# A message-passing layer on one core: hand order for VectorE and ScalarE too, both chunks' results written in their own pair, and the node-span product in two halves

## The chip, the core and the metric

The kernel runs on one core of a Trainium2 chip. The metric is the device time of one execution in microseconds. The core has TensorE (matrix products; a weight load, PEld in the profile, and a product, PE, are separate instructions), VectorE (DVE), ScalarE (ACT), GpSimd (POOL) and SyncE (SP). SP and ACT also issue ordinary DMAs, POOL issues the indirect ones. Products land in PSUM, which has eight banks of 2 KB per partition; everything else works in SBUF, which has 128 partitions.

## The reference

One layer of a graph network with 12,500 nodes, 32 features and 400,000 edges that are sorted by their destination:

```python
edge_index = jnp.stack([src, dst])
h = jnp.maximum(_layernorm(x, axis=-1), 0.0)
x = x + _L0_gnn_ref(h, edge_index, edge_attr_32, W1, b1, W2, b2)

# inside _L0_gnn_ref(x, ...), where x is h:
e_feat = jnp.concatenate([x[rol], x[col], edge_attr], axis=-1)   # rol = src, col = dst
h = jax.nn.relu(e_feat @ W1 + b1)                                # 96 -> 64
v = h @ W2 + b2                                                  # 64 -> 32
x_cand = jax.ops.segment_max(v, col, num_segments=num_nodes)
return jnp.maximum(x_cand, x[:, -v.shape[-1]:])
```

## The kernel before

The edges are cut into four stripes of 100,000 (`NS`), and each stripe into 196 chunks of 512 (`NCH`, `C`). A chunk index `c` means 512 edges of each of the four stripes, side by side on the partitions. The loop at L94 takes two chunks per turn; one turn is called a pair here, and there are 98.

For one pair the work is:

- **Source rows.** `gather(c)` (L139) fetches the rows `h[src]` by indirect DMAs on POOL, one for each 128 edges: 12 per chunk in nearly all chunks. The remaining 512 edges of a chunk get their rows from TensorE: `rows_by_matmul` (L278) builds one-hot matrices from node keys on DVE (`hot`, seven instructions at L285; `its`, one at L287) and multiplies them with the node table that lies in SBUF in two parts (`hs`). One **row tile** is one product at L292 and fourteen at L295, over 448 columns, into a bank of `pv`; DVE reduces it to rows by a maximum (L297, `gm`). There are four row tiles per chunk, so eight per pair, made for the chunks of the next pair. In this text the row tiles of a pair in the new order are called a0 to a3 and b0 to b3.
- **Features to partitions.** `to_features` (L322) transposes both kinds of rows into `ht` on DVE (L324 for gathered rows, L326 for computed ones). L324 is what frees a `gh` buffer for a later gather; there are six, three pairs' worth.
- **Hidden layer.** `into_ph` (L379) adds three groups of products into four banks `ph`: the edge attributes `ea`, a one-hot of the destination window `of` times the rows `qw` of node products, and `ht`. ScalarE applies bias and relu (L389, `hid`).
- **Second layer.** L399 makes `pv[0]` and `pv[1]`, the messages of the two chunks, and a scan on DVE (L404, `sm`) runs a maximum along the edges that starts anew at each node.
- **Leaving.** `leave_1` turns `sm` by four transposes (L336, `tr`), adds the bias (L338, `so`), and marks the last edge of each node in a window of 32 nodes per stripe (L340, `last`). `leave_2` multiplies the two (L350), so that the maxima fall on their nodes, copies the result on ScalarE (L353, `wo`) and writes it by four DMAs on SP (L357).

`load(c)` brings attributes, destinations and breaks of four chunks at a time and the `qw` rows (L318), two chunks ahead.

PSUM is full: four banks for `ph`, one for `tr`, and three for `pv`. The three `pv` banks go round in the order of allocation, over row tiles and messages alike:

```python
po = ps.tile([P, C], F32, name="pv", bufs=3)[:, :D * A0]
pv = [ps.tile([P, C], F32, name="pv", bufs=3) for x in range(2)]
```

Within the loop the order of instructions on SP and TensorE is that of the program (`manual_schedule` at L273). On DVE, ScalarE and POOL a planner chooses the order when the kernel is built; in the trace it runs L324 two pairs ahead of the pair that uses it. On every engine instructions then run in their fixed order, each waiting for its semaphores. The row tiles are strewn between the other products by `next(tiles)`, and the chunk c - 1 of the pair before leaves in the middle of a pair, beside chunk c.

Of the kernel before, what the change touches and what calls it, by code (L numbers as in the profile page):

```python
# [20 lines left out]
DVE = mybir.EngineType.DVE  # L21

P = 128
# [35 lines left out]
def gnn_kernel(ctx, tc, x, src, src_mm, src_t, dst, dst_next, dst_ext, lo, hi, edge_attr, weights, w1, w2, b2, out):  # L59
# [212 lines left out]
    with tc.tile_pool(name="edges", bufs=3) as pool, tc.tile_pool(name="edges_ps", bufs=1, space=PSUM) as ps, \  # L272
            tc.manual_schedule(engines={SP, PE}):  # L273
        loaded = {}
        windows = {}
        mm_rows = {}

        def rows_by_matmul():  # L278

            for i, c in enumerate(MMC):  # L280
                kb = pool.tile([P, 2, MM * P], F16, name="kb", bufs=2)
                nc.scalar.dma_start(kb, ap(key_d, i * MM * P, [[0, P], [len(MMC) * MM * P, 2], [1, MM * P]]))
                hot = pool.tile([P, A1, MM * P], F32R, name="hot", bufs=2)
                for k in range(A1):
                    nc.vector.tensor_scalar(hot[:, k], kb[:, 0], key_p[:, k:k + 1], None, op0=ALU.is_equal)  # L285
                its = pool.tile([P, MM * P], BF16, name="its", bufs=2)
                nc.vector.tensor_scalar(its, kb[:, 1], place, None, op0=ALU.is_equal)  # L287
                gm = mm_rows[c] = pool.tile([P, MM, D], F32, name="gm", bufs=6)
                for m in range(MM):
                    e = slice(m * P, (m + 1) * P)  # L290
                    po = ps.tile([P, C], F32, name="pv", bufs=3)[:, :D * A0]
                    nc.tensor.matmul(po, its[:, e], others.rearrange("p f a -> p (f a)"), start=True, stop=False)  # L292
                    for k in range(A1):
                        for part in range(2):
                            nc.tensor.matmul(po, hot[:, k, e], hs[:, part, k].rearrange("p f a -> p (f a)"),  # L295
                                             start=False, stop=(k == A1 - 1 and part == 1))
                    nc.vector.tensor_reduce(gm[:, m, :], po.rearrange("p (f a) -> p f a", a=A0),  # L297
                                            axis=AX.X, op=ALU.max)
                    yield
# [20 lines left out]

        def to_features(c, gh):
# [9 lines left out]

# [14 lines left out]
        def leave_2(c, so, last):  # L346
# [8 lines left out]
            for s in range(NS):  # L355
                g = slice(s * W, (s + 1) * W)
                nc.sync.dma_start(top_d[s % 2][bass.ds(base[s], W), :], wo[g, s * D:(s + 1) * D])  # L357
# [213 lines left out]
```

## Time and profile before

| | us |
|---|---|
| median of 3 runs | 5318.59 |
| lowest, highest | 5317.23, 5335.30 |
| profiled execution | 5227.3 (its span: 5225.5) |

| engine | busy us | share of span |
|---|---|---|
| TensorE products | 3638.2 | 70% |
| TensorE weight loads (beside products) | 2775.9 | 53% |
| POOL | 2238.9 | 43% |
| VectorE | 1846.3 | 35% |
| ScalarE | 315.6 | 6% |

The mean granted TensorE clock is 0.81 of the full one. The setup before the loop takes about 180 us of the span. A row of the profile names the line, the engine, the operation, the tiles it writes and reads, and how long the engine stood idle before it with what ended the wait; "issue" there means that it waited for nothing that the profile shows, "remote" that it names no instruction that ended the wait.

### The profile page before, as it was taken

The numbers are of one execution on the slowest core, as the hardware profiler recorded it, in microseconds if no ns is written. First come the engines' busy times: TensorE is split into PE (matmuls) and PEld (weight loads), VectorE is DVE, ScalarE is ACT, GpSimd is POOL, SyncE is SP. The second block draws the span as 40 slices with busy tenths as digits, with TensorE's granted clock in tenths as the row PEclk, the third lists the DMA queues.
The fourth block names the chain that finished last, engine by engine and source line by source line (L and its number), as shares of the span: only waits on it lengthen the run. The fifth ranks groups of instructions, "written<-read, shape, count | busy, mean of one in ns | idle before, by whom it ended". The sixth has DMA issues, their size and how long they took to land. (4 is left out here: it accounts for less than half of the span.)

```text
span 5225.5 us, 57318 instructions
## 1 busy us (share of the span) xinstructions
PE 3638.2 (70%) x20281; PEld 2775.9 (53%) x20281; DVE 1846.3 (35%) x3612; ACT 315.6 (6%) x627; POOL 2238.9 (43%) x2369
## 2 busy tenths in 40 slices
PE   2376767676767676767676767676767676777687
PEld 1255555555555555555554555555555555555565
DVE  2333333333333333333333333333333333333344
ACT  1000000000000000000000000000000000000000
POOL 6534344444444444444444444444444444444420
PEclk6587878787878787878788888787878787878788
DMA  3321112211211121112111211121112211211121
GB/s 123 90 58 43 42 39 58 44 41 40 58 42 41 40 56 44 40 40 56 44 40 40 57 44 40 40 56 44 41 40 57 44 41 40 57 44 40 40 53 65
DMA packets 235577, 256.47 MB, mean 49 GB/s; under 512 B 123653, under 2 KB 211861, under 8 KB 222102
## 3 DMA queue, kind: packets, MB, share of 16 engines
q10 hardware_dynamic: 74084, 137.60, 9.7%
q0 software_dynamic: 75296, 38.70, 5.6%
q1 hardware_dynamic: 85906, 76.48, 4.9%
q8 instruction: 159, 2.61, 0.2%
q14 instruction: 132, 1.08, 0.1%
HBM read 238.44 MB, written 14.04 MB: 48 GB/s over the span
## 5 line engine op out<-in xcount | busy, mean ns | idle before, releaser
L143 POOL DMA_INDIRECT gh<-h_d,src_i x2353 | 2234.8, 950 | 2812.1 <-DVE ht L324 2098.3
L295 PE MATMUL pv<-hs,hot 128*128 128x448 f32 x10808 | 2874.0, 413 | 712.6 <-issue 712.4
L295 PEld LDWEIGHTS pv<-hs,hot 128*128 128x128 f32 x10808 | 2282.8, 212 | 1444.9 <-issue 1270.9
L297 DVE TENSOR_REDUCE gm<-pv 128x32 f32<-128x448 f32 x772 | 481.2, 623 | 2548.3 <-remote 1529.4
L292 PE MATMUL pv<-others,its 128*128 128x448 bf16 x772 | 301.9, 391 | 427.0 <-issue 386.0
L285 DVE TENSOR_SCALAR hot<-kb,key_p 128x512 fp32r<-128x512 f16 x1351 | 555.8, 479 | 9.5 <-DMA qw<-q_d 9.5
L350 PE MATMUL tr<-so,last 128*128 128x128 f32 x1568 | 250.2, 282 | 250.0 <-issue 240.8
L404 DVE TENSOR_TENSOR_SCAN sm<-pb,sm,pv 128x512 f32<-128x512 bf16 x195 | 248.9, 1276 | 469.3 <-remote 332.5
L350 PEld LDWEIGHTS tr<-so,last 128*128 128x128 f32 x1568 | 227.1, 197 | 229.5 <-issue 211.8
L389 ACT ACTIVATE hid<-ph,wt 128x512 f32<-128x512 f32 x392 | 239.3, 690 | 973.5 <-PE ph L379 529.9
L292 PEld LDWEIGHTS <-its 128*128 128x128 bf16 x772 | 78.0, 101 | 400.5 <-issue 387.4
L353 ACT ACTIVATE wo<-tr 128x128 f32<-128x128 f32 x196 | 54.5, 278 | 3810.7 <-remote 1817.6
L336 PE MATMUL tr<-ident,sm 128*128 128x128 f32 x784 | 146.0, 319 | 22.3 <-ACT wo L353 22.3
L336 PEld LDWEIGHTS tr<-ident,sm 128*128 128x128 f32 x784 | 117.9, 167 | 57.9 <-ACT wo L353 38.4
L338 DVE TENSOR_TENSOR so<-tr,wt 128x512 f32<-128x512 f32 x196 | 133.9, 683 | 24.1 <-PE pv L292 11.5
L340 DVE TENSOR_TENSOR last<-iota_w,at 128x512 f32<-128x512 f32 x196 | 131.6, 672 | 28.2 <-PE tr L350 28.2
L324 DVE STREAM_TRANSPOSE ht<-gh 128x384 f32<-128x384 f32 (+1 forms) x196 | 102.9, 563 | 71.0 <-PE ph L379 54.8
L379 PE MATMUL ph<-ea,wt 32*64 32x512 f32 x1568 | 110.0, 617 | 8.4 <-DMA ea<-in_edge_attr 8.4
L379 PE MATMUL ph<-ht,wt 32*64 32x512 f32 x1568 | 110.9, 612 | 0.5 <-issue 0.4
L379 PE MATMUL ph<-of,qw 32*64 32x512 f32 x1568 | 105.5, 592 | 6.2 <-issue 6.2
L399 PE MATMUL pv<-hid,wt 64*32 64x512 f32 x1568 | 108.9, 604 | 0.2 <-ACT hid L389 0.2
L287 DVE TENSOR_SCALAR its<-kb,place 128x512 bf16<-128x512 f16 x193 | 69.6, 361 | 96.4 <-remote 80.1
(68 smaller groups left out, 399.3 us busy)
## 6 DMA issues: line engine op xcount, KB each, us to landing
ea<-in_edge_attr SPq DMA_DIRECT2D x49, 1024.0 KB
db<-in_dst_ext ACTq DMA_DIRECT2D x196, 256.0 KB
kb<-key_d ACTq DMA_DIRECT2D x193, 256.0 KB
gh<-h_d,src_i POOLq DMA_INDIRECT x2353
pb<-pen_d ACTq DMA_DIRECT2D x196, 128.0 KB
qw<-q_d SPq DMA_DIRECT2D x784, 8.0 KB
top_d<-wo SPq DMA_DIRECT2D x784, 4.0 KB
top_d<-zero ACTq DMA_DIRECT2D x2, 1568.0 KB
```

Source lines behind the costliest of these rows:

```text
L143: nc.gpsimd.indirect_dma_start(out=gh[:, k, :], out_offset=None, in_=h_d[:, :], in_offset=bass.IndirectOffsetOnAxis(ap=src_i[:, c, k:k + 1 ...
L285: nc.vector.tensor_scalar(hot[:, k], kb[:, 0], key_p[:, k:k + 1], None, op0=ALU.is_equal)
L292: nc.tensor.matmul(po, its[:, e], others.rearrange("p f a -> p (f a)"), start=True, stop=False)
L295: nc.tensor.matmul(po, hot[:, k, e], hs[:, part, k].rearrange("p f a -> p (f a)"), start=False, stop=(k == A1 - 1 and part == 1))
L297: nc.vector.tensor_reduce(gm[:, m, :], po.rearrange("p (f a) -> p f a", a=A0), axis=AX.X, op=ALU.max)
L336: nc.tensor.transpose(px[:, j, :], sm[:, j * P:(j + 1) * P], ident)
L338: nc.vector.tensor_tensor(so, px, b2r[:, None, :].to_broadcast([P, J, P]), op=ALU.add)
L340: nc.vector.tensor_tensor(last, iota_w[:, None, None, :].to_broadcast([P, J, NS, W]), at[:, :, c * J:(c + 1) * J].rearrange("p s j -> p j ...
L350: nc.tensor.matmul(pw, last[:, j].rearrange("p s w -> p (s w)"), so[:, j, :], start=(j == 0), stop=(j == J - 1))
L379: nc.tensor.matmul(ph[s][x * HID:(x + 1) * HID], w[g], e[g], start=start, stop=stop)
L389: nc.scalar.activation(hid[s], ph[s], AF.Relu, bias=b1c)
L404: nc.vector.tensor_tensor_scan(sm, loaded.pop(c + x)[2], pv[x], before, op0=ALU.add, op1=ALU.max)
```

## The change

DVE and ScalarE join SP and TensorE in the hand order, so that their instructions run as the loop is written. The generator `rows_by_matmul` becomes three functions: `load_keys` (the DMA of keys, on ScalarE's queue), `one_hots` (the eight DVE instructions, in whole or in part) and `tile_by_matmul` (the products), which hands its reduction back to be placed later by `select()`. `of` and `last` get functions of their own, `window_hots` and `lasts`. In the loop the gathers stand ahead of the loads, each reduction has its place after a row tile, and both chunks of a pair leave in that pair. The product in `leave_2` covers, instead of 128 by 128 with only the diagonal blocks used, two halves of 64 by 64 columns into two halves of the partitions; the copy to `wo` is 64 columns wide. `sm` has three buffers instead of four.

```diff
@@ -19,6 +19,7 @@
 SP = mybir.EngineType.SP
 PE = mybir.EngineType.PE
 DVE = mybir.EngineType.DVE
+ACT = mybir.EngineType.Activation
 
 P = 128
 N = 12500
@@ -270,33 +271,48 @@
 
     ea_v = edge_attr.rearrange("s f e -> (s f) e")
     with tc.tile_pool(name="edges", bufs=3) as pool, tc.tile_pool(name="edges_ps", bufs=1, space=PSUM) as ps, \
-            tc.manual_schedule(engines={SP, PE}):
+            tc.manual_schedule(engines={SP, PE, DVE, ACT}):
         loaded = {}
         windows = {}
+        ofs = {}
+        keys = {}
+        hots = {}
         mm_rows = {}
 
-        def rows_by_matmul():
-
-            for i, c in enumerate(MMC):
-                kb = pool.tile([P, 2, MM * P], F16, name="kb", bufs=2)
-                nc.scalar.dma_start(kb, ap(key_d, i * MM * P, [[0, P], [len(MMC) * MM * P, 2], [1, MM * P]]))
-                hot = pool.tile([P, A1, MM * P], F32R, name="hot", bufs=2)
-                for k in range(A1):
-                    nc.vector.tensor_scalar(hot[:, k], kb[:, 0], key_p[:, k:k + 1], None, op0=ALU.is_equal)
-                its = pool.tile([P, MM * P], BF16, name="its", bufs=2)
-                nc.vector.tensor_scalar(its, kb[:, 1], place, None, op0=ALU.is_equal)
-                gm = mm_rows[c] = pool.tile([P, MM, D], F32, name="gm", bufs=6)
-                for m in range(MM):
-                    e = slice(m * P, (m + 1) * P)
-                    po = ps.tile([P, C], F32, name="pv", bufs=3)[:, :D * A0]
-                    nc.tensor.matmul(po, its[:, e], others.rearrange("p f a -> p (f a)"), start=True, stop=False)
-                    for k in range(A1):
-                        for part in range(2):
-                            nc.tensor.matmul(po, hot[:, k, e], hs[:, part, k].rearrange("p f a -> p (f a)"),
-                                             start=False, stop=(k == A1 - 1 and part == 1))
-                    nc.vector.tensor_reduce(gm[:, m, :], po.rearrange("p (f a) -> p f a", a=A0),
-                                            axis=AX.X, op=ALU.max)
-                    yield
+        def load_keys(c):
+            if c in MMC:
+                kb = keys[c] = pool.tile([P, 2, MM * P], F16, name="kb", bufs=2)
+                nc.scalar.dma_start(kb, ap(key_d, (c - MMC.start) * MM * P,
+                                           [[0, P], [len(MMC) * MM * P, 2], [1, MM * P]]))
+
+        def one_hots(c, groups):
+
+            if c not in MMC:
+                return
+            if c not in hots:
+                hots[c] = (pool.tile([P, A1, MM * P], F32R, name="hot", bufs=2),
+                           pool.tile([P, MM * P], BF16, name="its", bufs=2))
+            hot, its = hots[c]
+            for k in groups:
+                nc.vector.tensor_scalar(hot[:, k], keys[c][:, 0], key_p[:, k:k + 1], None, op0=ALU.is_equal)
+            if A1 - 1 in groups:
+                nc.vector.tensor_scalar(its, keys.pop(c)[:, 1], place, None, op0=ALU.is_equal)
+
+        def tile_by_matmul(c, m):
+            if c not in MMC:
+                return
+            if m == 0:
+                mm_rows[c] = pool.tile([P, MM, D], F32, name="gm", bufs=6)
+            hot, its = hots[c]
+            e = slice(m * P, (m + 1) * P)
+            po = ps.tile([P, C], F32, name="pv", bufs=3)[:, :D * A0]
+            nc.tensor.matmul(po, its[:, e], others.rearrange("p f a -> p (f a)"), start=True, stop=False)
+            for k in range(A1):
+                for part in range(2):
+                    nc.tensor.matmul(po, hot[:, k, e], hs[:, part, k].rearrange("p f a -> p (f a)"),
+                                     start=False, stop=(k == A1 - 1 and part == 1))
+            rows = mm_rows[c][:, m, :]
+            return lambda: nc.vector.tensor_reduce(rows, po.rearrange("p (f a) -> p f a", a=A0), axis=AX.X, op=ALU.max)
 
         def load(c):
             if c % LOAD == 0:
@@ -318,6 +334,10 @@
                 nc.sync.dma_start(qw[s * W:(s + 1) * W, :], q_d[bass.ds(base[s], W), :])
             windows[c] = qw, base
 
+        def window_hots(c):
+            of = ofs[c] = pool.tile([P, C], F32, name="of", bufs=4)
+            nc.vector.tensor_scalar(of, loaded[c][1], node[:, c:c + 1], None, op0=ALU.is_equal)
+
         def to_features(c, gh):
             ht = pool.tile([P, K, D], F32, name="ht", bufs=4)
             n = min(K - MM * (c in MMC), (SE - c * C) // D)
@@ -329,6 +349,14 @@
                 nc.vector.memset(ht[:, n:], 0.0)
             return ht.rearrange("p k e -> p (k e)")
 
+        def lasts(c):
+            last = pool.tile([P, J, NS, W], F32, name="last", bufs=2)
+            nc.vector.tensor_tensor(
+                last, iota_w[:, None, None, :].to_broadcast([P, J, NS, W]),
+                at[:, :, c * J:(c + 1) * J].rearrange("p s j -> p j s")[:, :, :, None].to_broadcast([P, J, NS, W]),
+                op=ALU.is_equal)
+            return last
+
         def leave_1(c, sm):
 
             px = ps.tile([P, J, P], F32, name="tr")
@@ -336,38 +364,35 @@
                 nc.tensor.transpose(px[:, j, :], sm[:, j * P:(j + 1) * P], ident)
             so = pool.tile([P, J, P], F32, name="so", bufs=2)
             nc.vector.tensor_tensor(so, px, b2r[:, None, :].to_broadcast([P, J, P]), op=ALU.add)
-            last = pool.tile([P, J, NS, W], F32, name="last", bufs=2)
-            nc.vector.tensor_tensor(
-                last, iota_w[:, None, None, :].to_broadcast([P, J, NS, W]),
-                at[:, :, c * J:(c + 1) * J].rearrange("p s j -> p j s")[:, :, :, None].to_broadcast([P, J, NS, W]),
-                op=ALU.is_equal)
-            return so, last
+            return so
 
         def leave_2(c, so, last):
 
-            pw = ps.tile([P, J, P], F32, name="tr")[:, 0]
+            pw = ps.tile([P, J, P], F32, name="tr")[:, 0, :2 * D]
             for j in range(J):
-                nc.tensor.matmul(pw, last[:, j].rearrange("p s w -> p (s w)"), so[:, j, :],
-                                 start=(j == 0), stop=(j == J - 1))
-            wo = pool.tile([P, P], F32, name="wo")
+                for g in range(2):
+                    nc.tensor.matmul(pw[g * 2 * W:(g + 1) * 2 * W],
+                                     last[:, j, 2 * g:2 * g + 2].rearrange("p s w -> p (s w)"),
+                                     so[:, j, g * 2 * D:(g + 1) * 2 * D], start=(j == 0), stop=(j == J - 1))
+            wo = pool.tile([P, 2 * D], F32, name="wo")
             nc.scalar.activation(wo, pw, AF.Copy)
             _, base = windows.pop(c)
             for s in range(NS):
                 g = slice(s * W, (s + 1) * W)
-                nc.sync.dma_start(top_d[s % 2][bass.ds(base[s], W), :], wo[g, s * D:(s + 1) * D])
-
-        tiles = rows_by_matmul()
+                nc.sync.dma_start(top_d[s % 2][bass.ds(base[s], W), :], wo[g, s % 2 * D:(s % 2 + 1) * D])
+
+        load_keys(MMC.start)
         for c in range(AHEAD):
             load(c)
+            window_hots(c)
+        one_hots(MMC.start, range(A1))
         sm = None
         for c in range(0, NCH, 2):
+            a, b = c + 2, c + 3
+            gh = [gather(c + x) for x in range(2)]
+            load_keys(b)
             for k in range(c + AHEAD, min(c + AHEAD + 2, NCH)):
                 load(k)
-            gh = [gather(c + x) for x in range(2)]
-            of = []
-            for x in range(2):
-                of.append(pool.tile([P, C], F32, name="of", bufs=4))
-                nc.vector.tensor_scalar(of[x], loaded[c + x][1], node[:, c + x:c + x + 1], None, op0=ALU.is_equal)
 
 
             ph = [ps.tile([P, C], F32, name=f"ph{s}") for s in range(NS)]
@@ -378,20 +403,34 @@
                     for x, (w, e) in enumerate(pairs):
                         nc.tensor.matmul(ph[s][x * HID:(x + 1) * HID], w[g], e[g], start=start, stop=stop)
 
+            waiting = []
+
+            def tile(c, m):
+                waiting.append(tile_by_matmul(c, m))
+
+            def select():
+                f = waiting.pop(0)
+                if f:
+                    f()
+
             into_ph([(w1c, loaded[c + x][0]) for x in range(2)], True, False)
-            into_ph([(windows[c + x][0], of[x]) for x in range(2)], False, False)
-            next(tiles, None)
+            into_ph([(windows[c + x][0], ofs.pop(c + x)) for x in range(2)], False, False)
+            tile(a, 0)
             ht = [to_features(c + x, gh[x]) for x in range(2)]
             into_ph([(w1a, ht[x]) for x in range(2)], False, True)
             hid = []
             for s in range(NS):
                 hid.append(pool.tile([P, C], F32, name="hid", bufs=6))
                 nc.scalar.activation(hid[s], ph[s], AF.Relu, bias=b1c)
-            next(tiles, None)
-            next(tiles, None)
-
-            if c > 0:
-                left = leave_1(c - 1, sm)
+            select()
+            one_hots(b, range(A1))
+            load_keys(a + 2)
+            tile(a, 1)
+            select()
+            last = [lasts(c)]
+            tile(a, 2)
+            select()
+            last.append(lasts(c + 1))
             pv = [ps.tile([P, C], F32, name="pv", bufs=3) for x in range(2)]
             for s in range(NS):
                 for x in range(2):
@@ -400,19 +439,27 @@
             sms = []
             for x in range(2):
                 before = -LOW if sm is None else sm[:, C - 1:C]
-                sm = pool.tile([P, C], F32, name="sm", bufs=4)
+                sm = pool.tile([P, C], F32, name="sm", bufs=3)
                 nc.vector.tensor_tensor_scan(sm, loaded.pop(c + x)[2], pv[x], before, op0=ALU.add, op1=ALU.max)
                 sms.append(sm)
-            next(tiles, None)
-            next(tiles, None)
-            if c > 0:
-                leave_2(c - 1, *left)
-            next(tiles, None)
-            left = leave_1(c, sms[0])
-            next(tiles, None)
-            leave_2(c, *left)
-            next(tiles, None)
-        leave_2(NCH - 1, *leave_1(NCH - 1, sm))
+            tile(a, 3)
+            select()
+            so = leave_1(c, sms[0])
+            tile(b, 0)
+            select()
+            one_hots(a + 2, range(4))
+            leave_2(c, so, last[0])
+            tile(b, 1)
+            select()
+            so = leave_1(c + 1, sms[1])
+            one_hots(a + 2, range(4, A1))
+            tile(b, 2)
+            select()
+            leave_2(c + 1, so, last[1])
+            for k in range(a, min(a + 2, NCH)):
+                window_hots(k)
+            tile(b, 3)
+            select()
 
 
     with tc.tile_pool(name="out", bufs=1) as pool:
```

## The prediction

> **What bounds the kernel now.** Four views, in this order. First the page's busy shares and slices:
>
> ```profile
> PE 3638.2 (70%) x20281; PEld 2775.9 (53%) x20281; DVE 1846.3 (35%) x3612; ACT 315.6 (6%) x627; POOL 2238.9 (43%) x2369
> PE   2376767676767676767676767676767676777687
> PEclk6587878787878787878788888787878787878788
> POOL 6534344444444444444444444444444444444420
> ```
>
> TensorE is busiest, but seven tenths in nearly every slice. Only where POOL runs dry, at the end, does it fill up. Second, windows inside one pair, and one pair after the last gather (columns: stretch and its length, then busy us and instructions of PE, weight loads, DVE, ACT, POOL; then clock, DMA share, GB/s):
>
> ```profile
> 2624.00:2630.00 6.00, 6.00 (x38) 5.02 (x45) 1.65 (x4) 1.53 (x3) 4.66 (x5) 1.00 0.10 15
> 2630.00:2653.00 23.00, 12.17 (x62) 8.39 (x47) 3.36 (x5) 0.00 (x0) 17.21 (x20) 0.80 0.10 14
> 2653.00:2676.00 23.00, 19.19 (x115) 14.68 (x116) 13.10 (x29) 1.03 (x3) 0.84 (x1) 0.76 0.27 75
> 5107.00:5138.00 31.00, 31.00 (x209) 25.15 (x209) 18.25 (x37) 2.90 (x6) 0.00 (x0) 1.00 0.17 46
> ```
>
> Without gathers a pair takes 31.2 us and TensorE never stops. With them the pairs follow each other every 52.2 us (first gathers at 280.1 and 5030.8, 91 steps). So 21 us of each pair are lost, and most of it in the 23 us in which POOL gathers: 62 products. Third, the timeline of that stretch:
>
> ```profile
> 2621.96 1.11 PE L379 MATMUL ph<-ht,wt 32*64 32x512 f32 x16
> 2623.27 1.05 DVE L324 STREAM_TRANSPOSE ht<-gh 128x384 f32<-128x384 f32 x2 [0.58 <-PE ph L379]
> 2624.12 0.94 POOL L143 DMA_INDIRECT gh<-h_d,src_i  x1 [21.87 <-DVE ht L324]
> ...
> 2630.69 3.13 PE L295 MATMUL pv<-hs,hot 128*128 128x448 f32 x14
> ...
> 2635.41 0.35 PE L292 MATMUL pv<-others,its 128*128 128x448 bf16 x1 [1.59 <-issue]
> ...
> 2650.17 0.53 PE L295 MATMUL pv<-hs,hot 128*128 128x448 f32 x1 [1.57 <-issue]
> ...
> 2652.98 0.62 DVE L297 TENSOR_REDUCE gm<-pv 128x32 f32<-128x448 f32 x1 [15.24 <-remote]
> ```
>
> The row tile issued from 2630.65 ends at 2633.8 by its records, yet its reduction starts at 2652.98, 19 us later; elsewhere a reduction follows its tile by 0.04 us. TensorE's completions arrive late while gathers run, about one per 0.7 us (load or product alike, whatever its size), and issue stops some 60 instructions ahead. Counted from a burst's first gather (91 bursts alike): results are prompt until +6, late until +33.8 (median), and the burst starts because the two transposes of gathered rows (L324) free the buffers. In the late stretch TensorE goes on only as far as no instruction needs a late result. Today the third row tile (issued at +6.5), the fourth (+13.1 on average), and the fifth (+22.4) get out.
>
> **The change, part by part.** A pair is summed from the burst's first gather, at 0.
>
> *Where the burst falls.* Today DVE runs L324 two pairs ahead, just after the products from `ht`. In the new order L324 follows the reduction of the pair's last row tile. So the first gather comes 0.04 + 0.62 (L297) + 0.58 (L324) + 0.27 (L324's end to the gather) = 1.5 us after that tile. TensorE from there: `ea` and `of` 1.9 (2616.89 to 2618.79), tile a0 3.17, `ht` 1.04: done at +4.6, in time. Tile a1 from +4.6 to +7.6 is caught: 14 of its 30 instructions by +6, the other 16 at 0.7: +17.2. Tile a2 is issued behind it. Then the products into `pv`: the second chunk's bank is a1's (three `pv` banks in rotation), so they wait for a1's reduction: all issued by +18.9. Tile a3 takes a2's bank. 30 more completions at 0.7 would be +38.2, so it comes with the flush at +33.8, and a3 starts at +34.5. Rest of the pair: five tiles at 3.02 = 15.1, two transposes at 0.59 = 1.2, two node-span products 2.3 (below) = 18.6. The clock stays at 0.5 for 3 to 7 us after a stall (resumed 2606.3, full by 2609; 2657.9, by 2665): 2.5 us lost. Last tile ends at +55.6, next burst at +57.1. The same sum today: after +33.8 come half a tile, a transpose, tile, spans, tile, `ea`, `of`, tile, `ht`, with the clock 18.4: 52.2. Queued behind the waiting reduction of a1 on DVE are `lasts`, a2's reduction, both scans; TensorE waits for these only through the banks.
>
> Here the Trainium skill speaks against the row ("SBUF — State Buffer", section Who interferes with whom): it says that TensorE and ScalarE never wait on anyone, and that DMA does not contend with compute. By that rule where the gathers fall costs nothing and the pair would stay at 52.2 plus the span products. The windows above decide: 62 products in 23 us beside gathers, 209 in 31 without.
>
> *One-hots beside gathers.* `one_hots(b)`, eight DVE instructions, moves to +4.4, into the burst. The trace has that once, at the start:
>
> ```profile
> 188.40 2.86 DVE L285 TENSOR_SCALAR hot<-kb,key_p 128x512 fp32r<-128x512 f16 x7 [9.48 <-DMA qw<-q_d]
> 191.29 3.39 POOL L143 DMA_INDIRECT gh<-h_d,src_i  x1 [0.30 <-issue]
> 191.58 0.55 PE L292 MATMUL pv<-others,its 128*128 128x448 bf16 x1 [11.39 <-DVE its L287]
> 213.71 0.62 DVE L297 TENSOR_REDUCE gm<-pv 128x32 f32<-128x448 f32 x1 [19.16 <-PE pv L295]
> ```
>
> A gather took 3.39 instead of 0.95: the three beside sixteen such instructions lost 2.8 us, so eight lose 1.4; five at 242.18 cost one gather 0.3, so eight 0.5. The same section's rule, that an instruction in a two-port mode shuts GpSimd out for its whole length, would make it 8 x 0.4 = 3.2. I take 1.0, nearer the rows; ends 0.5 and 3.2. Against it I set 0.4: in a tenth of the bursts the late tile came at +28.9 or sooner, where a2 would be free before the flush.
>
> *Halved span products.* Out: 8 loads and products of 128 columns, 0.88 us (a tile with them takes 3.90, without 3.02). In: 16 of each with 64 columns. Nearest row: the 16 `pv` products (L399), also in column groups, take 1.02 us from first issue to the next tile, of which 2 x 0.21 is streaming; so 0.6 is entering and leaving. With 0.2 to 0.85 for the work that is 0.8 to 1.45: -0.1 to +0.6 each. I take +0.25 (in the 2.3 above). Their 32 extra instructions per pair lie after +38, where completions are prompt; in the late stretch each would cost 0.7.
>
> *Edits at no cost.* ScalarE order: four relus, two copies and the key loads, 6% busy. Both key loads are issued before they are needed: chunk b's some 4 us ahead of the pair, chunk a+2's after the relus, 15 us before use; the load at 2609.77 took under 4 us. Without that cover b's one-hots slip, and b0 needs them only at +38. SP: eight result writes now lie in one pair (9.7 us at 2606.89), and the next span loads queue behind them, a pair early. Gathers standing ahead of loads changes no queue: POOL has only gathers. `lasts` (2 x 0.67) and `of` (2 x 0.43) fill DVE's idle time under tiles; `sm` with three buffers is read out within its pair; the copy of 64 columns (under 0.28) is under a tile of 3.
>
> *Sum.* A pair: 57.1 + 1.0 - 0.4 = 57.7, against 52.2: +5.5 x 91 = +500. L324 is no longer two pairs ahead, so bursts also fall in two pairs that now run free: 2 x (57.7 - 31.2) = +53. Pair 0 (83.2 from its first tile to pair 1's, beside left-over gathers) becomes like the rest: -25. Together +528 on the profiled execution's 5227.3: 5755. The median, 5318.6, is 1.0175 times that execution; scaled, 5855.
>
> **The rivals.**
>
> *Faster: the late stretch is opened by the `pv` products, not by time.* In all 91 bursts these come at +5.5 to +6.5, so the steady trace can't separate the two. For it: the first late results are theirs. Then the new order keeps TensorE free until they end at +11.7, and as today 9.3 us of work gets out in the late stretch: 33.8 + (31.7 - 11.7 - 9.3) + 2.5 = 47.0 per pair, -5.2 x 91 + 32 - 36 = -477, scaled 4835. It decides if a1 and a2 are reduced promptly. Against: the tile at 191.58, before any `pv` product, was 19 us late.
>
> *Nothing but the span products.* If the late stretch hides as much as today wherever it lies, a pair gains -0.2 to +1.2: 5300 to 5430, near 5345. For it: DVE is idle two thirds of the span. Against: a3 needs a2's bank.
>
> *Worse: `ht` caught too.* Late from +4.6 would put the relus and `pv` behind the flush: +1.8 per pair, about 6025. Results at +5.6 were prompt, so I doubt it. That the change doesn't do what it says is unlikely: the order is the program's.
>
> **How the numbers follow.** Burst shift as summed 0.64 (own range 5650 to 6070: 3.3 to 7.8 us per pair); `pv` opens it 0.18; spans only 0.13, half of it within 0.5%; others 0.05. About 0.5%, 27 us, is what a measurement here tells from no change. Slower 0.74, same 0.06, faster 0.20. The range, 5020 to 6080, takes the first and third case and the upper edge of the second.
>
> **What would show it.** Right: L324 right after the last row tile's reduction, the first gather 1.5 us after that tile; a1's reduction near +17, a2's near +34, `pv` products issued around +18, then a long gap on TensorE; pairs near 57.7; POOL's wait for L324 longer per pair; free pairs near 31.7. Wrong: a1 and a2 reduced within 0.1 us of their ends; three row tiles issued between +6 and +34; gathers faster or interleaved with other work.

## The result and the profile after

| | median us (runs) | profiled execution |
|---|---|---|
| before | 5326.94 (4: 5317.23 to 5336.05) | 5227.3, clock 0.81 |
| after | 5673.98 (4: 5667.73 to 5676.80) | 5676.8 (span 5675.0), clock 0.76 |

The ratio is 1.065, with a 95% interval of 1.062 to 1.068: slower, where 5855 had been predicted and the range was 5020 to 6080. By the two profiled executions the kernel lost 449.5 us, by the medians 347: the profiled execution before lies almost 2% below the median before, and why is not known. Later runs landed on other chips. On one of them the very same two kernels take 3194 and 3251 us, ratio 1.018, and on another the kernel before takes 3192: TensorE's results come promptly there beside gathers. So each experiment below says whether results were prompt or late where it ran, and is compared with the kernel before on that chip.

The page of the changed kernel, shares and slices:

```profile
PE 3746.6 (66%) x21849; PEld 2569.8 (45%) x21849; DVE 1829.6 (32%) x3612; ACT 329.9 (6%) x627; POOL 2281.9 (40%) x2369
PE   2476767675767676757675767676767676767676
PEclk6687878787878787878787777777778777777778
POOL 5334343434443434343434343434343434343431
```

TensorE's share fell from 70% to 66%, and its last slices no longer fill up: POOL has gathers until the end. Windows of one pair after, cut at the burst's first gather, at the point where results come late, and at the flush (columns as in the windows before):

```profile
2628.85:2634.60 5.75, 5.75 (x53) 4.02 (x38) 0.61 (x3) 0.00 (x0) 4.53 (x5) 1.00 0.70 209
2634.60:2663.00 28.40, 10.36 (x27) 5.00 (x26) 3.63 (x9) 2.75 (x4) 18.63 (x20) 0.62 0.26 64
2663.00:2685.90 22.90, 22.21 (x161) 17.32 (x161) 13.78 (x26) 0.45 (x2) 0.00 (x0) 0.88 0.07 13
```

Before, 62 products were counted in 23 us of the late stretch. Now there are 27 in 28.4 us. Behind the flush TensorE is busy to 97%, so nothing is lost there. The timeline shows what the 28.4 us wait for:

```profile
2628.01 0.57 DVE L344 STREAM_TRANSPOSE ht<-gh 128x384 f32<-128x384 f32 x1
...
2628.85 0.94 POOL L144 DMA_INDIRECT gh<-h_d,src_i  x1 [25.95 <-DVE ht L346]
...
2632.36 1.11 PE L404 MATMUL ph<-ht,wt 32*64 32x512 f32 x16
...
2633.45 3.13 PE L312 MATMUL pv<-hs,hot 128*128 128x448 f32 x14
...
2634.57 0.62 DVE L315 TENSOR_REDUCE gm<-pv 128x32 f32<-128x448 f32 x1 [5.14 <-PE ph L404]
...
2640.19 0.69 ACT L424 ACTIVATE hid<-ph,wt 128x512 f32<-128x512 f32 x1 [15.54 <-DMA qw<-q_d]
...
2654.58 0.69 ACT L424 ACTIVATE hid<-ph,wt 128x512 f32<-128x512 f32 x1 [7.76 <-issue]
...
2663.01 0.62 DVE L315 TENSOR_REDUCE gm<-pv 128x32 f32<-128x448 f32 x1 [24.78 <-remote]
...
2663.68 1.96 PE L438 MATMUL pv<-hid,wt 64*32 64x512 f32 x14 [6.78 <-DVE gm L315]
...
2665.62 4.46 PE L312 MATMUL pv<-hs,hot 128*128 128x448 f32 x14
```

The first gather starts at 2628.85. Row tile a0 ended at 2632.4, and its reduction is already 2.1 us late (2634.57). The products from `ht` end at 2633.5; their first relu starts at 2640.19, their last at 2654.58. (Ahead of that first relu ScalarE also issued loads, until 2639.83; but pairs without these loads have it no sooner.) Tile a1 (2633.45) is reduced at 2663.01, with the flush, 26 us after its end. `pv[1]` needs that bank, so its products and a3 stand behind the flush, as the prediction called the moment when the held-back results all come. (The gather's row names L346; the buffer is freed by L344, which ends at 2628.58.) Over 80 pairs of the middle (means, from the first gather):

| | predicted | after |
|---|---|---|
| first gather behind the pair's first product | 1.5 behind the last tile | 1.49 (before: 7.23) |
| a0's reduction | in time, +4 | +7.8 |
| first and last relu | in time, by +7 | +13.9, +29.1 |
| a1's reduction | +17.2 | +34.1 |
| last product into `pv` issued | +18.9 | +35.8 |
| a3 issued | +34.5 | +36.7 |
| last gather starts | +29.8 (+29.3 to +32.0) | +29.3 (before: +28.8) |
| step from pair to pair | 57.7 | 56.9 (before: 52.2) |

### The profile page after: what moved, and what is told of

The parts are those of the page before. It is cut to its first block, busy times and chain, and to the rows that moved or that the text cites. A ratio compares the mean times of both kernels' runs of the same rounds, so it can differ in the third digit from the quotient of the medians.

```text
span 5675.0 us, 60305 instructions
## 1 busy us (share of the span) xinstructions
PE 3746.6 (66%) x21849; PEld 2569.8 (45%) x21849; DVE 1829.6 (32%) x3612; ACT 329.9 (6%) x627; POOL 2281.9 (40%) x2369
## 5 line engine op out<-in xcount | busy, mean ns | idle before, releaser
L312 PE MATMUL pv<-hs,hot 128*128 128x448 f32 x10808 | 2911.0, 405 | 1128.6 <-issue 1126.4
L144 POOL DMA_INDIRECT gh<-h_d,src_i x2353 | 2277.8, 968 | 3272.5 <-DVE ht L346 2500.5
L312 PEld LDWEIGHTS pv<-hs,hot 128*128 128x128 f32 x10808 | 2205.3, 205 | 1560.4 <-issue 1419.8
L438 PE MATMUL pv<-hid,wt 64*32 64x512 f32 x1568 | 329.1, 1032 | 565.3 <-DVE gm L315 395.3
L424 ACT ACTIVATE hid<-ph,wt 128x512 f32<-128x512 f32 x392 | 264.2, 687 | 3021.1 <-remote 1693.6
L438 PEld LDWEIGHTS pv<-hid,wt 64*32 64x32 f32 x1568 | 40.7, 134 | 775.9 <-DVE gm L315 528.8
L378 ACT ACTIVATE wo<-tr 128x64 f32<-128x64 f32 x196 | 43.8, 223 | 2192.1 <-PE tr L374 2189.4
L374 PE MATMUL tr<-so,last 128*64 128x64 f32 x3136 | 134.8, 228 | 3.8 <-DVE so L366 3.8
L374 PEld LDWEIGHTS tr<-so,last 128*64 128x64 f32 x3136 | 107.6, 138 | 62.6 <-issue 57.9
L364 PE MATMUL tr<-ident,sm 128*128 128x128 f32 x784 | 117.4, 272 | 2.0 <-DVE sm L443 1.4
L344 DVE STREAM_TRANSPOSE ht<-gh 128x384 f32<-128x384 f32 (+1 forms) x196 | 108.3, 553 | 0.3
```

The lines of the kernel that those rows point to most:

```text
L144: nc.gpsimd.indirect_dma_start(out=gh[:, k, :], out_offset=None, in_=h_d[:, :], in_offset=bass.IndirectOffsetOnAxis(ap=src_i[:, c, k:k + 1 ...
L364: nc.tensor.transpose(px[:, j, :], sm[:, j * P:(j + 1) * P], ident)
L374: nc.tensor.matmul(pw[g * 2 * W:(g + 1) * 2 * W], last[:, j, 2 * g:2 * g + 2].rearrange("p s w -> p (s w)"), so[:, j, g * 2 * D:(g + 1) * ...
L424: nc.scalar.activation(hid[s], ph[s], AF.Relu, bias=b1c)
L438: nc.tensor.matmul(pv[x][s * D:(s + 1) * D], w2x[g], hid[s][g], start=True, stop=True)
```

## The experiments

Until e9 the theory was the prediction's: the burst's place in the pair decides how much TensorE gets out while its results are late. The rivals: the loss is in another part of the hand order, or products in row and column groups open the late stretch.

**e1: no gathers.** Prompt results.

```diff
-            gh = [gather(c + x) for x in range(2)]
+            gh = [first_gather(c + x) for x in range(2)]   # rows of chunk 2 for chunks 3 to 194
```

> The changed kernel with the gathers of all chunks but the first three and the last left out: those chunks take the rows gathered for chunk 2, so values are wrong in them, work and order are the same. If gathers are what makes TensorE's results late: no late results, TensorE busy throughout, a pair at 31.0 us (31.2 free before, less 0.2 for the span products), 93 x (56.9 - 31.0) = 2410 us gone, about 3270 us. If the order written by hand is itself what costs (scans, one-hots or maxima that come too late on VectorE): a pair stays well above 33 us and the time above 3500 us.

It took 3184.7 us (one execution), but the kernel before took 3191.8 beside it: results are prompt there with all gathers in place, so this says nothing on why they come late elsewhere. It bounds what gathers cost where results are prompt: against the changed kernel's 3251 on a like chip 66 us, about 2%. All of it lies in every second pair, the one with the loads of `db` and `pb` (31.7 against 33.1 us, see e5); the other pairs take 30.71 us with and without gathers.

**e2 and e11: transposes of the next pair hoisted.** The same kernel twice; e2 with prompt results, e11 with late ones.

```diff
-            ht = [to_features(c + x, gh[x]) for x in range(2)]           # L344 and L346 of this pair
+            ht = [to_features(c + x, hts.pop(c + x)) for x in range(2)]  # L346 alone
             into_ph([(w1a, ht[x]) for x in range(2)], False, True)
+            for k in range(a, min(a + 2, NCH)):
+                hts[k] = gathered_features(k, gh.pop(k))                 # L344 of the next pair
```

> The changed kernel with one thing undone: VectorE transposes the gathered rows of the next pair right behind the products from ht, as the scheduler had placed it, so the burst of gathers starts some 6 us later in the pair. If the burst's place is the cause: pairs at 52.2 - 0.2 (span products) + 0.5 (one-hots beside gathers) = 52.5 us, so 5676.8 - 93 x 4.4 = about 5270 us, within 1% of the kernel before. If the loss is another part of the hand-written order (one-hots, both maxima in one pair, ScalarE's order): pairs stay near 56.9 us, 5650 us or more.

> The changed kernel with the burst of gathers back behind the products from ht and nothing else undone (as in e2_burst_back), in the hope of late results, under which it has not run. With late results, if the burst's place in the pair is what the change lost: pairs near 52.2 - 0.4 (halves) + 0.5 (one-hots beside gathers) = 52.3 us and a time within 1.5% of the kernel before. If it is another part of the hand order that loses there: pairs near 56.9 us, ratio over 1.05. With prompt results: ratio 1.017 again, which tells nothing new.

e2: ratio 1.0166 (1.0151 to 1.0182), which tells nothing of the place, as no result was late. e11: 5612.7 against 5221.5, ratio 1.075 (1.069 to 1.082), 56.2 us a pair. By what was expected of it e11 speaks against the theory, but its timeline shows that the edit did not do what it was made for:

```profile
2630.13 1.04 DVE L344 STREAM_TRANSPOSE ht<-gh 128x384 f32<-128x384 f32 x2
2630.97 0.94 POOL L144 DMA_INDIRECT gh<-h_d,src_i  x1 [25.67 <-DVE ht L344]
```

In VectorE's order nothing ahead of these two transposes waits for the products from `ht`, so the burst came 2.0 us behind the pair's first product, against 1.5 in the changed kernel and 7.2 before. So e11 is a near repeat of the changed kernel and not the test of the place. It is of use as a control: to transpose a pair ahead, with the burst left where it was, changes little (56.2 against 56.9 us a pair).

**e3: the halves alone, in the kernel before.** Prompt results.

```diff
-                nc.tensor.matmul(pw, last[:, j].rearrange("p s w -> p (s w)"), so[:, j, :], ...)
+                for g in range(2):
+                    nc.tensor.matmul(pw[g * 2 * W:(g + 1) * 2 * W], last[:, j, 2 * g:2 * g + 2]..., ...)
```

> The kernel before with the span products in halves and nothing else changed. From the traces of before and after, a row tile with a span product behind it is followed by the next tile 0.12 us sooner: 2 x 0.12 x 98 = 24 us less, ratio 0.9955. By the prediction's estimate, +0.25 us each: 49 us more, ratio 1.009. If the 32 extra instructions of a pair wait in the late stretch at 0.7 us each: over 1.05.

3207.1 against 3191.8, ratio 1.0048 (1.0034 to 1.0061): slower, between the two numbers written down (0.9955 and 1.009), but for neither's reason. By pairs it comes apart. Pairs without the loads of `db` and `pb` fell from 31.15 (e8) to 30.73 us, so the halves gain 0.42. Every second pair, the one with those loads, rose from 31.2 to 32.1. VectorE's waits for gathered rows in e3, and below it in e8 (total us, times, longest):

```profile
DVE ht L324 <- DMA gh<-h_d,src_i: 335.4, 93, 11.4
DVE ht L324 <- DMA gh<-h_d,src_i: 225.4, 107, 14.1
```

In the planner's order L324 runs two pairs ahead, and VectorE stands there for rows that are still to come. POOL never stops in e3: a gather starts every 1.31 us, 24 take 31.4 us, and the mean pair takes 31.44 us. So POOL sets the pace, and what stands on VectorE behind L324 waits with it. In the second pairs VectorE stands 5.9 us before L324 (2.4 in the others), the reduction of the second row tile comes at +12.8 instead of +9.6 us from the pair's start, and the fourth tile, which needs a bank, starts 1.3 us later. That fits the 1.4 us by which these pairs are longer; an edit that removes the wait alone was not run.

**e4: a second row tile ahead of the products from `ht`.** Prompt results.

```diff
             tile(a, 0)
+            tile(a, 1)
             ht = [to_features(c + x, gh[x]) for x in range(2)]
```

> The changed kernel with the second row tile (a1) issued ahead of the products from ht, so TensorE has two tiles of 128x128 products, and no product in row groups, from 0.4 to 6.6 us after the burst's first gather. If late results begin by time, near +3.3: a1's reduction is late as well (after +9, where its tile ends near +6.7). If products in row or column groups open them: a0 and a1 are reduced within 1 us of their ends (before +8), and only what comes from ht on is late. The pair in both near 57 us, for the same three tiles get out before the flush.

3245.6 us (one execution), and no late result at all: inconclusive for what it was made for.

**e5 and e8: both kernels again.** Prompt results, on another chip.

> The changed kernel itself, again, because the four runs before took 3192 to 3249 us where the two kernels had taken 5319 and 5674: TensorE's results came promptly there although the gathers took the same 0.94 us each. If that was the chip's doing and it holds here: about 3245 us against 3192, ratio 1.017 (each second pair 2.3 us longer than its neighbour: its relus start 6 us late, behind eight loads on ScalarE's queue). If results come late again: 5674 against 5327, ratio 1.065.

> The kernel before itself, for a profile of it beside these runs. With prompt results: pairs of 30.7 us (the step of every other pair with the span products in halves), less or more by the halves, 3192 us. With late results: 52.2 us a pair as in the profile shown, 5319 us.

3250.9 against 3194.1, ratio 1.018 (1.016 to 1.020), and 3194.3 for e8. A gather takes the same 0.94 us every 1.25 us and TensorE is 95 and 96% busy. There the loss is elsewhere. The timeline of e5, a pair with the loads and the next without:

```profile
1490.27 0.48 ACTq L326 DMA_DIRECT2D db<-in_dst_ext  x1
...
1492.68 1.11 PE L404 MATMUL ph<-ea,wt 32*64 32x512 f32 x16
...
1497.68 1.11 PE L404 MATMUL ph<-ht,wt 32*64 32x512 f32 x16
...
1504.01 0.43 ACTq L327 DMA_DIRECT2D pb<-pen_d  x1
1504.49 1.27 ACT L424 ACTIVATE hid<-ph,wt 128x512 f32<-128x512 f32 x2 [14.52 <-issue]
...
1525.48 1.11 PE L404 MATMUL ph<-ea,wt 32*64 32x512 f32 x16
...
1530.48 1.11 PE L404 MATMUL ph<-ht,wt 32*64 32x512 f32 x16
1531.63 0.69 ACT L424 ACTIVATE hid<-ph,wt 128x512 f32<-128x512 f32 x1 [8.85 <-PE ph L404]
```

The products from `ht` are done at 1498.8, but the relu starts at 1504.49, right behind the eighth of the loads on ScalarE's queue. In the next pair, which has no such loads, it follows its products by 0.04 us. The pair with loads takes 32.80 us (1492.68 to 1525.48). Over the middle pairs the steps are 33.1 and 30.7, against 31.2 and 31.15 in e8, where the planner had put the four loads of `db` among the relus and the four of `pb` behind them.

**e6: those loads behind the relus.** Prompt results.

```diff
-                for s in range(NS):                       # in load(c), ahead of the relus
-                    nc.scalar.dma_start(db[g, :n], ...); nc.scalar.dma_start(pb[g, :n], ...)
+                later.append(by_scalar)                   # the same eight loads
...
                 nc.scalar.activation(hid[s], ph[s], AF.Relu, bias=b1c)
+            while later:
+                later.pop()()
```

> The changed kernel with one thing moved: ScalarE's eight loads of db and pb, which every second pair issues ahead of its relus, are issued behind the relus. With prompt results: if those loads are what costs in each second pair, its step falls from 33.1 to about 30.8 us, 49 x 2.3 = 113 us, to some 3135 us, 2% under the kernel before. If the cost in those pairs comes from another thing of every second pair (the 1 MB load of ea on SyncE, or DMA traffic), nothing moves, 3245 us. With late results: pairs with and without these loads took 57.0 and 56.7 us, so at most 49 x 0.3 = 15 us less than 5674.

3133.2 against 3194.1, ratio 0.981 (0.979 to 0.983), 2 us from the 3135 expected. All pairs now take 30.71 us; the same pair as above in e6:

```profile
1501.47 1.11 PE L410 MATMUL ph<-ea,wt 32*64 32x512 f32 x16
...
1506.47 1.11 PE L410 MATMUL ph<-ht,wt 32*64 32x512 f32 x16
1507.62 1.27 ACT L430 ACTIVATE hid<-ph,wt 128x512 f32<-128x512 f32 x2 [8.86 <-DMA qw<-q_d]
1508.22 0.34 ACTq L329 DMA_DIRECT2D db<-in_dst_ext  x1
...
1532.18 1.11 PE L410 MATMUL ph<-ea,wt 32*64 32x512 f32 x16
```

So with prompt results the whole loss was these eight loads, and without them the change gains 1.9%. Of these 61 us some 43 are the 0.44 us a pair that the halves also give in e3's undisturbed pairs: the order by hand itself makes the steady pair no shorter there.

**e7: gathers in six groups of four.** Prompt results. Buffers of four gathers, freed one by one by a transpose behind each of six row tiles' reductions.

```diff
-        gh = gathered.tile([P, K, D], F32, name="gh")                  # bufs=6
+            if k % PART == 0:                                          # PART = 4, bufs=18
+                parts.append(gathered.tile([P, PART, D], F32, name="gh"))
...
             select()
+            free()                                                     # behind a0, a1, a2, a3, b0, b1
```

> The changed kernel with the gathers in six groups of four per pair in place of one burst of 24: gathered buffers of four gathers, each freed by its own transpose, behind the reductions of row tiles a0, a1, a2, a3, b0 and b1. With late results: if it takes some 3 to 6 us of unbroken gathers to open the late stretch, groups of 5 us with gaps stay below it and pairs fall well under 50 us; if any gather delays TensorE's results, the pair stays at 52 us or more. With prompt results: no change beyond 1% of the changed kernel, since the gathers cost TensorE nothing there.

3241.3 (one execution), 0.3% under e5: nothing, as expected with prompt results.

**e9: loads behind the relus, span products whole.** From here on results came late, on two further chips.

> The kernel with the loads behind the relus (3133 us), with the span products whole again, 128 columns, as they were before the change. If the halves are worth what the steps of undisturbed pairs say (31.15 us before, 30.71 after): 98 x 0.43 = 42 us more, about 3175 us, ratio 0.994 to the kernel before. If the hand order itself brought that step down and the halves nothing: 3133 us, ratio 0.981. If results come late here: some 5650 us, and the two cannot be told apart to this precision.

5685.2 against 5247.0, ratio 1.083 (1.081 to 1.086). For the halves a row tile with a span product behind it gives a number here too: 3.96 us to the next tile, against 3.75 in the profile of after, 0.21 for each of the two. Moving the loads gained next to nothing there: 57.0 us a pair, some 0.4 of it for the whole products, against 56.9, while e9 had its relus at +8 to +19 in place of +14 to +29. Relus that come 6 to 10 us sooner do not help as long as a1 comes with the flush (+33.1).

**e10: groups of four, loads behind the relus.** Late results.

> The kernel with the loads behind the relus, and its gathers in six groups of four per pair. With prompt results: 3133 us within 0.5%, for the gathers hold nothing up there. With late results: if groups of four stay below what opens the late stretch, well under 5000 us; if any gather delays TensorE's results, 5200 us or more.

4395.6 in one execution against 5247.0: 16% faster than the kernel before, 43.1 us a pair. The groups often ran together all the same: in the middle pairs POOL made 115 runs of 4 gathers, 43 of 12 and 56 of 16 (6 were of 8). Windows of some 42 us of it:

```profile
2319.73:2330.79 11.06, 11.06 (x100) 7.34 (x98) 5.32 (x14) 0.30 (x2) 3.98 (x4) 1.00 0.42 129
2330.79:2345.90 15.11, 14.76 (x99) 12.10 (x99) 9.57 (x19) 2.35 (x4) 11.04 (x11) 1.00 0.61 136
2345.90:2362.00 16.10, 5.23 (x22) 3.92 (x21) 4.13 (x10) 0.22 (x1) 9.64 (x10) 0.73 0.08 11
```

In the first window POOL makes one group of four and stops for 6.2 us: TensorE never waits. From 2336.93 the groups run into each other, since two reductions had come 1.3 us apart, and 16 gathers follow without a break:

```profile
2330.66 3.13 PE L315 MATMUL pv<-hs,hot 128*128 128x448 f32 x14
...
2335.82 0.62 DVE L318 TENSOR_REDUCE gm<-pv 128x32 f32<-128x448 f32 x1 [2.29 <-remote]
...
2341.96 0.62 DVE L318 TENSOR_REDUCE gm<-pv 128x32 f32<-128x448 f32 x1 [0.32 <-PE tr L376]
...
2350.49 0.62 DVE L318 TENSOR_REDUCE gm<-pv 128x32 f32<-128x448 f32 x1 [5.70 <-PE pv L315]
...
2356.11 0.95 POOL L146 DMA_INDIRECT gh<-h_d,src_i  x1 [0.30 <-issue]
2359.84 0.62 DVE L318 TENSOR_REDUCE gm<-pv 128x32 f32<-128x448 f32 x1 [6.95 <-remote]
```

The group of four at 2330.79 already delays a result: tile a1 ends at 2333.8 and is reduced at 2335.82, 2.0 us late, and so close to a2's reduction. TensorE loses little by it (14.76 of 15.11 us busy). The reduction at 2341.96, 5 us into the run of 16, starts 0.9 us after its tile's end. The next one, of a tile that was issued at 2341.36 and needs 3.1 us, comes at 2350.49, 6 us late. The flush is 2.8 us after the end of the last gather. Over all pairs a tile that ends within a group of four is reduced 2.8 us after its end at most, one within a run of 16 up to 11.6 us. So short groups keep the delay small; they don't remove it.

**e12: the burst where it was.** Late results. e11's edit in the right place, behind a wait for TensorE, with the loads behind the relus.

```diff
             select()                                       # reduction of a0, behind the relus
+            for k in range(a, min(a + 2, NCH)):
+                hts[k] = gathered_features(k, gh.pop(k))   # L344 of the next pair
             one_hots(b, range(A1))
```

> The kernel with the loads behind the relus, and VectorE's transposes of the next pair's gathered rows behind the reduction of row tile a0, so that the first gather comes some 7 us after the pair's first product, where it came in the kernel before (in e11 it came at 2.0 us, against 1.5 us in the changed kernel: that edit had hardly moved it). With late results: if the burst's place is what the change lost, 52.3 us a pair and a ratio of 1.00 to 1.02. If it lost the order of the chain (the products into pv, scan, transposes and span products of one pair now follow each other with tiles b0 to b3 queued behind them, where a pair's second chunk left one pair later): only a3 and b0 get out before the flush at +33.8, then 18.3 us of work and 2.5 of clock, 55.3 us a pair or more, ratio 1.06 or more. With prompt results: 3133 us again, ratio 0.981.

5071.6 against 5222.6, ratio 0.970 (0.966 to 0.974); 50.5 us a pair. The burst now starts 6.5 us behind the pair's first product. Its windows, up to the flush:

```profile
2643.91:2649.90 5.99, 5.99 (x37) 5.05 (x43) 4.54 (x12) 2.09 (x4) 4.77 (x5) 1.00 0.28 58
2649.90:2677.90 28.00, 14.93 (x79) 10.23 (x63) 4.88 (x6) 0.00 (x0) 18.55 (x20) 0.72 0.09 12
```

79 products get out in the late stretch in place of 27. The timeline says why:

```profile
2649.58 1.09 PE L455 MATMUL pv<-hid,wt 64*32 64x512 f32 x16
...
2650.64 3.13 PE L313 MATMUL pv<-hs,hot 128*128 128x448 f32 x14
...
2652.56 2.66 DVE L460 TENSOR_TENSOR_SCAN sm<-pb,sm,pv 128x512 f32<-128x512 bf16 x2 [1.65 <-remote]
...
2654.41 3.13 PE L313 MATMUL pv<-hs,hot 128*128 128x448 f32 x14
...
2663.23 1.12 PE L382 MATMUL tr<-so,last 128*64 128x64 f32 x16 [5.69 <-DVE so L374]
```

Relus, a1 and a2 are through before results are late. The products into `pv` are issued at +5.7, a3 at +6.7, b0 at +10.5, the first span product at +19.3, b1 behind it. The changed kernel has the last products into `pv` at +35.8 and the other four behind +36. e9 and e12 differ by the place of L344 and by the halves. The halves are worth 0.4 us a pair, so about 6 of the 6.5 us between 57.0 and 50.5 are the place; that L344 is hoisted at all is not it (e11). The rival of e12 (the chain of one pair, with b0 to b3 behind it) fell. The gain is larger than expected, 50.5 us a pair for 52.3: against the kernel before, 0.7 us of it lies ahead of the burst and 1.0 behind its start. Why was not tried.

## Why the prediction was right, and where it was not

**Where the burst falls.** Right in the place (first gather 1.5 us after the last row tile's end, measured 2628.85 against 2627.4), in the direction, and shown by e12 to be the cause: put back, the pair falls from 57.0 to 50.5 us, 0.4 of it by the halves. Two times in the sum failed. `ht` was not "in time": its relus came at +13.9 to +29.1, which is in part the rival "`ht` caught too" (it had them behind the flush). And a1 was not reduced at +17.2. The step "14 of its 30 instructions by +6, the other 16 at 0.7" took a mean rate for a schedule, and a fixed start: in the changed kernel a0, which ended at +3.6, was already reduced some 4 us late. Tile a1's result came with the flush, at +34.1, in e9 (+33.1) as in the changed kernel; in e11 the median is +32. The two misses together cost 2.2 us, since the products into `pv` now stand between the flush and a3 (+36.7 for the predicted +34.5); the rival had put +1.8 on it. They cost no more because the sum had put a3 behind the flush anyway. And the pair's end hid them: the rest of the pair, below, was 2.4 us shorter than summed. That the step came within 0.8 us of the sum is in part luck.

**The rest of the pair.** From a3's issue to the end of the last tile it took 18.7 us, not 21.1. Two terms were too large. *Clock:* the first tile after the flush cost 0.95 us more than its work (4.56 to the next issue, transposes included, against 3.02 + 0.59), and the later ones nothing; 2.5 was summed. *Span products:* 3.75 from tile to tile, so 0.73 each with everything around it, where 0.88 + 0.25 was taken. The nearest row had been the products into `pv`, also in column groups. (The 0.21 us of streaming in that sum stands in no row of theirs; the tiles' products, of 448 columns, start 0.20 to 0.21 us apart.) The measured row is L374, for sixteen, against L350's for eight (after, then before):

```profile
2673.51 0.69 PE L374 MATMUL tr<-so,last 128*64 128x64 f32 x16
2612.91 1.05 PE L350 MATMUL tr<-so,last 128*128 128x128 f32 x8
```

e9 with whole products shows 0.21 each between the two, and e3 and e8 show 0.42 a pair with prompt results.

**One-hots beside gathers.** 1.0 was taken between 0.5 and 3.2. The burst grew from 28.8 to 29.3 us: the lower end, that of the five one-hots at 242.18. The rule of the Trainium skill ("SBUF — State Buffer", section Who interferes with whom), which made it 3.2, is far from the trace of this case. Its sentence that TensorE never waits on anyone closes a list on the ports of SBUF. Taken further, as the prediction tried it, it fits the two chips with prompt results, where TensorE is 95 to 96% busy beside gathers, and not the others: e9 and e12 differ by 614 us, nearly all by where the gathers lie.

**Edits at no cost.** Here a step was missing. ScalarE's order was costed as "four relus, two copies and the key loads"; its queue also has eight loads of `db` and `pb` in every second pair, and the hand order put them ahead of the relus. With late results this hides behind the flush (steps of 57.0 and 56.8 us with and without loads, e9 no faster). With prompt ones it is 2.4 us in every second pair and turns a gain of 1.9% into a loss of 1.8% (e6, e5).

**The sum and the scale.** Predicted were 5755 for the profiled execution, measured 5676.8: 78 us less, which is 93 bursts of 0.8 us. Then 5755 was multiplied by 1.0175, because the median before lay that much above its profiled execution. After, the profiled execution lies on the median (5676.8, 5674.0). This factor was the larger error, 100 of the 181 us.

**The rivals.** "Nothing but the span products" fell by the result with late results. "The `pv` products open the late stretch" fell too: in the changed kernel results were late before any of them was issued. In e12 they left at +5.7 and the scan behind them waited 1.65 us only. A lower granted clock is no cause of late results either: it is 1.00 in the window in which a0's result is already late (2628.85 to 2634.60), and falls afterwards.

**What stays open.** Why some chips deliver results late beside gathers and others do not: gathers, transfers and kernels were the same. Also why a0 was reduced later in the changed kernel (+7.8) than in e9 and e11 (+5.2, +3.9); the loads ahead of the relus don't explain it by themselves, for in pairs without them a0 came later still (+9.7 against +5.7). Products in row groups (e4) could not be tested where it counts. Nor was the kernel without gathers run where results come late. That unbroken gathers bring late results out rests on e10, on e12 and on the pairs behind the last gather, which take 31.15 us in the kernel before on its late chip. They are not enough for it: in e6 and e8 POOL gathers without a stop through the whole loop, and nothing is late.

## What to carry to other kernels

When a kernel's stalls come from an engine off the critical path, what frees that engine's buffers is a scheduling decision of its own: moving two transposes, and the burst with them, by 5 us changed this kernel by some 10% where results come late (e9, e12). Cutting the burst of 24 gathers into groups of four, though many ran together again, brought another 13% in one execution (e12, e10). When an engine's order is written by hand, list everything in its queue, loads issued from it included, and put issues that may string out (13.7 us for eight) behind what others wait for. And take the same two kernels to a second chip before believing a ratio: here the sign held, but the cause was another one.

## What had not been expected of the hardware

- The same program takes 3192 to 3194 us on two chips and 5221 to 5327 on others, with gathers of equal length (0.94 us each). The only difference found is when TensorE's results are seen by the engines that wait for them: where they are prompt, a reduction that VectorE stands ready for starts 0.04 us behind its tile in every middle pair, elsewhere up to 26 us behind.
- Late results come beside a run of gathers, and the delay builds up: a tile that ends 5 us into the run is reduced at once in the kernel before and in e12, one that ends at +3.6 is 3.6 us late (median) in the changed kernel, and from +10 on every one is late in all of these runs. The held-back results are there together some 3 to 4 us after the end of the last gather.
- Where results are prompt, POOL is next: 24 gathers take 31.2 us in e6 (one every 1.30) without a stop, a pair takes 30.7, and only the lead of three pairs covers it. In e3, which needs the rows two pairs sooner, POOL sets the pace already.
- Eight DMA issues on ScalarE, 0.31 to 0.48 us each, can hold that engine for 13.7 us (1490.27 to 1504.01). What they wait for was not tested. It is not the gathers alone: without them (e1) the eight still start 12.7 us apart from first to last, against 13.9 in e5 (means).
